# Cross-attention in float32: the output product as three single-pass products of upper parts, remainders and scaled differences

## The chip, the cores and the metric

One core of a Trainium2 chip runs the whole kernel. The metric is device microseconds of one execution, as the median of several. The kernel before takes 573.02 us (three runs, 572.77 to 575.41).

## The reference, cut to what matters

Everything is float32. The input x is (2, 2048, 640), the context is (2, 128, 384) with 124 text tokens and 4 adapter tokens for each of the two batches, and there are 8 heads of 80.

```python
query = hidden_states @ Wq
keyt, valt = enc @ Wk, enc @ Wv
hs = _mha(query, keyt, valt)                      # text attention
ca_q1 = jnp.einsum('btc,th->bch', ca, Wq_ca)[:, indices, :]
ca_hs1 = _mha(ca_q1, residual, residual)          # 384 adapter queries over 2048 tokens
ca_q2 = ca_hs1 @ Wq
ca_hs2 = _mha(ca_q2, ca @ Wk_ca, ca @ Wv_ca)
out = (hs + ca_hs2) @ Wout + b_out + residual
```

The change is in `hs @ Wout`: 4096 rows by 640 by 640. The adapter's part of the output product and the bias are made apart, as rows o2 of 384 for each batch, and gathered onto the output rows by an indirect DMA that adds.

## The kernel before, in words

**Units and stages.** The 4096 tokens are eight blocks of 512 for the queries and sixteen units of 256 (two tiles of 128) for everything behind. For unit m, `text_scores` (L2140) makes the scores sc, `softmax` (L2178) the probabilities, which go to HBM (kept) and come back turned, as pT (`probabilities`, L2242). `hidden` (L2365) multiplies pT with the values into PSUM (ph): the attention output of 256 tokens, turned, so that its 640 features lie on the partitions in five chunks of 128. `text_out_fast` (L2392) copies ph to SBUF (hs) and multiplies with Wout into PSUM (po). VectorE adds each finished half row of po (128x320) onto x, which `residual` (L2330) has loaded into a row tile. `stored` (L2508) lets GpSimd's queue gather-add the o2 rows (`add_second`, L2349) and then writes the rows to the output. `adapter` (L1869) runs beside this: for each batch 24 groups of scores s, of which VectorE takes the maxima mx, then 24 groups of scores whose exponentials ea ScalarE makes, contracted into acc (`contract`, L1985); `second` (L2030) ends it with o2.

**The output product before.** `by_columns` (L402) issues one 128-row product as four matmuls with weights of 128x32, one to each 32 columns of the array; they run at the same time. A float32 matmul is two matmul instructions in the trace. Of the five chunks of 128 features, four are multiplied by Winograd's form of Strassen's scheme: each unit has seven products of half size instead of eight. It needs sums of the hidden state (s1 to s4, written by VectorE or GpSimd into hs) and of Wout (t1 to t4, `sums_of_wout`, L2311). The seven products are 14 calls of `by_columns`, and the fifth chunk is 4 more: 18 for each unit. They stand in four chains, and eight adds of 128x320 on VectorE take them out.

**Who sets the order.** Every step is a `Do` that names its engine and its work. A class `Desk` (L67) issues the steps one by one in the order of a table, `TURNS` (L85): each task has a path of numbers, and each of its steps a turn. The remainder of a turn by 6 names the engine (0 TensorE, 1 ScalarE, 2 VectorE, 3 GpSimd, 4 SyncE, 5 none), and the turns count upwards through the program, so the turns divisible by 6, read in order, are TensorE's instruction stream. Each engine's queue runs strictly in that order. Path .55 is the adapter of the first batch, .55.1 that of the second (its end, `second`, is .55.1.3), and .56 to .71 are units 0 to 15; under a unit, .3 is `probabilities` with `hidden` in its last steps.

**Rooms.** A `Room` counts buffers; a step that needs one waits until it is free. Those of the late part: 4 PSUM banks m0 to m3 and 4 more (quad) for the adapter's scores; two rooms for pT, one in the slot of an old x block (`take_pT`, L2282); eight row tiles for x and the output rows (x_more and last_rows, `take_rows`, L2271); three sets for hs (`take_hs`, L2290).

**Shapes of the array.** Products with 128 rows and 32 columns (po, pq, ph, acc), 64 rows and 128 columns (sc), 32 rows and 128 columns (s) and the full 128 by 128 follow each other. The operands of s and of a part of sc are float32r (`F32R`), which is one matmul instruction for each product, on operands cut to fewer bits.

## Time and profile before

| | |
|---|---|
| time, median of 3 | 573.02 us |
| span of the profiled execution, first to last instruction | 571.3 us |
| its own time | recorded only as the span; the median is 1.7 us above it |
| TensorE busy | 563.6 us (99%) in 8069 matmul instructions |
| VectorE, ScalarE, GpSimd busy | 394.4, 286.7, 159.8 us |
| granted TensorE clock | 1.000 |
| DMA | 113.21 MB, mean 198 GB/s |

How to read it: a busy TensorE row says that matmul instructions follow each other without a gap, and their modelled ends overlap. What one product costs is the distance from its start to the start of the next, which the timeline shows, not the duration in a group's row. A row of the groups reads: line, engine, operation, output<-inputs, shape, count | busy us, mean ns of one | idle us before it and what ended it. The 128*32 ahead of a matmul's operands is the part of the array that it uses.

### The profile page before, as it was taken

The numbers are of one execution on the slowest core, as the hardware profiler recorded it, in microseconds if no ns is written. First come the engines' busy times: TensorE is split into PE (matmuls) and PEld (weight loads), VectorE is DVE, ScalarE is ACT, GpSimd is POOL, SyncE is SP. The second block draws the span as 40 slices with busy tenths as digits, with TensorE's granted clock in tenths as the row PEclk, the third lists the DMA queues.
The fourth block names the chain that finished last, engine by engine and source line by source line (L and its number), as shares of the span: only waits on it lengthen the run. The fifth ranks groups of instructions, "written<-read, shape, count | busy, mean of one in ns | idle before, by whom it ended". The sixth has DMA issues, their size and how long they took to land.

```text
span 571.3 us, 18875 instructions
## 1 busy us (share of the span) xinstructions
PE 563.6 (99%) x8069; PEld 310.0 (54%) x8069; DVE 394.4 (69%) x659; ACT 286.7 (50%) x806; POOL 159.8 (28%) x213
## 2 busy tenths in 40 slices
PE   9999999999999999999999999999999999999997
PEld 8885335455555455466554554554555554445553
DVE  4366999999998577458999999998332213544443
ACT  2021355645566899899876654524554664100000
POOL 9102041114440731100004350531203053045152
PEclk9999999999999999999999999999999999999999
DMA  8998576965968977446746969977476587799888
GB/s 246 211 248 126 139 161 157 172 179 139 211 212 153 215 182 211 146 126 198 233 158 203 316 180 319 245 217 230 96 263 120 164 206 223 248 211 213 258 156 237
DMA packets 145691, 113.21 MB, mean 198 GB/s; under 512 B 82548, under 2 KB 116980, under 8 KB 145608
## 3 DMA queue, kind: packets, MB, share of 16 engines
q1 hardware_dynamic: 137000, 95.10, 60.0%
q0 software_dynamic: 5632, 10.69, 11.7%
q10 hardware_dynamic: 2976, 6.23, 3.2%
q8 instruction: 63, 1.03, 0.8%
q14 instruction: 20, 0.16, 0.1%
HBM read 71.60 MB, written 40.39 MB: 196 GB/s over the span
## 4 chain that ended last, share of the span: by engine, by line
PE 92%; DVE 3%; ACT 3%; DMA 1%; issue 1%; SPq 0%; ACTq 0%; DVEq 0%
PE po L405 27%; PE pq L405 24%; PE sc L396 7%; PE acc L396 7%; PE s L396 7%; PE ph L396 6%; PE pq L396 4%; PE pyz L396 2%; ACT ea L427 2%; DVE mx L427 2%; PE pv L396 1%; PE pk L396 1%; DMA xz<-in_x_dram 1%; ACT p L427 1%; PE pt_wq L410 1%
## 5 line engine op out<-in xcount | busy, mean ns | idle before, releaser
L427 ACT ACTIVATE p<-sc,m 128x124 f32<-128x124 f32 x256 | 90.1, 381 | 43.4 <-DVE m L427 38.4
L427 DVE TENSOR_REDUCE mx<-s 128x4 f32<-128x2048 f32 x48 | 109.0, 2271 | 1.9 <-PE s L396 1.9
L427 ACT ACTIVATE ea<-s 128x2048 f32<-128x2048 f32 x48 | 90.5, 1884 | 31.4 <-PE s L396 30.9
L405 PE MATMUL po<-wout_sums,hs 128*32 128x320 f32 x1024 | 78.5, 434 | 0.1
L405 PE MATMUL po<-wout_sb,hs 128*32 128x320 f32 x928 | 72.4, 433 | 0.0
L427 POOL TENSOR_TENSOR p<-p,r 128x992 f32<-128x992 f32 x17 | 31.4, 1847 | 130.9 <-DVE r L427 130.9
L405 PE MATMUL pq<-xt,wq_sb 128*32 128x256 f32 (+1 forms) x928 | 66.4, 418 | 0.0
L427 DVE TENSOR_TENSOR last_rows<-last_rows,po 128x320 f32<-128x320 f32 x60 | 28.1, 480 | 44.0 <-PE po L405 43.9
L427 ACT ACTIVATION_READ_ACCUMULATOR p<-sc,m 128x1 f32 x256 | 57.0, 223 | 0.0
L427 DVE TENSOR_TENSOR x_more<-x_more,po 128x320 f32<-128x320 f32 x68 | 32.4, 481 | 34.5 <-PE po L405 32.5
L405 PEld LDWEIGHTS po<-wout_sums,hs 128*32 128x32 f32 x1024 | 33.4, 110 | 32.7 <-issue 2.8
L427 DVE TENSOR_REDUCE m<-sc 128x4 f32<-128x496 f32 x64 | 40.8, 663 | 14.1 <-PE sc L396 14.0
L396 PE MATMUL acc<-ea,y_sb 128*32 128x384 f32 (+2 forms) x768 | 50.2, 382 | 0.2 <-ACT ea L427 0.2
L396 PE MATMUL ph<-pT,vpad 128*32 128x256 f32 x768 | 47.9, 381 | 0.0
L405 PEld LDWEIGHTS po<-wout_sb,hs 128*32 128x32 f32 x928 | 30.1, 110 | 28.2 <-issue 1.6
L2351 POOL DMA_INDIRECT x_more<-o,query x17 | 26.6, 1563 | 67.0 <-DVE x_more L427 31.1
L405 PEld LDWEIGHTS pq<-xt,wq_sb 128*32 128x32 f32 x928 | 27.7, 110 | 28.0 <-issue 13.4
L427 ACT COPY hs<-ph 128x512 f32<-128x512 f32 (+1 forms) x25 | 13.4, 551 | 57.7 <-PE ph L396 57.7
L427 DVE STREAM_TRANSPOSE eb<-p 128x1024 f32<-128x1024 f32 x32 | 39.4, 1233 | 1.2 <-POOL p L427 1.1
L396 PEld LDWEIGHTS sc<-kmain,q 64*128 64x128 f32 x512 | 31.8, 187 | 12.6 <-issue 5.8
L427 POOL TENSOR_TENSOR hs<-hs 128x256 f32<-128x256 f32 x31 | 28.9, 1019 | 33.9 <-ACT hs L427 25.6
L396 PE MATMUL sc<-kmain,q 64*128 64x124 f32 x512 | 38.0, 285 | 0.0
(219 smaller groups left out, 835.0 us busy)
## 6 DMA issues: line engine op xcount, KB each, us to landing
kept<-eb SPq DMA_DIRECT2D x32, 512.0 KB
pT<-kept SPq DMA_DIRECT2D x16, 1024.0 KB
landing<-away SPq DMA_DIRECT2D x15, 512.0 KB
xi<-in_x_dram SPq DMA_DIRECT2D x56, 128.0 KB
x_more<-in_x_dram SPq DMA_DIRECT2D x17, 320.0 KB
last_rows<-in_x_dram SPq DMA_DIRECT2D x15, 320.0 KB
y<-yt SPq DMA_DIRECT2D x16, 256.0 KB
y_sb<-y SPq DMA_DIRECT2D x32, 128.0 KB
```

The costliest lines, as they stand in the source:

```text
L396: self.pin(self.nc.tensor.matmul(out, lhsT, rhs, **kw))
L405: self.pin(self.nc.tensor.matmul(out[j : j + 32], lhsT[:, j : j + 32], rhs, **kw))
L410: self.pin(self.nc.tensor.transpose(out, in_, ident))
L427: self.pin(getattr(engine, what)(*args, **kw))
L2351: desk.pin(nc.gpsimd.indirect_dma_start(out=t, out_offset=None, in_=o2_of[b], in_offset=bass.IndirectOffsetOnAxis(ap=query[:, st : st + 1] ...
```

## The change

The output product of a tile k of 128 tokens is now made with float32r matmuls on the full array. The hidden state a is split into an upper part h (its low 12 bits cleared) and the remainder l = a - h, and Wout the same way into wh and wl. With e = 2^-12, three products are summed: h·wh and l·(wl/e) into one PSUM bank, and (e·h - l)·(e·wh - wl) into another. VectorE adds (1 + e) times the first and -1/e times the second onto the row tile, which is h·wh + h·wl + l·wh + l·wl.

For each unit that is 2 tiles x 2 halves of the columns x 5 chunks x 3 products = 60 matmuls of 128x128 weights and 320 columns; a chain's step e0 has ten of them, its step e1 five. Ahead of them stand, for each of the two tiles, a masking on VectorE, two copies on ScalarE (one scaled) and two subtractions of 128x640 on GpSimd or VectorE; the sums s1 to s4 go. `parts_of_wout` replaces `sums_of_wout`: it loads the five chunks of Wout twice more and splits them.

Rooms: one for pT instead of two; five row tiles instead of eight; a room for the raw hidden state (raws); four sets of 128 tokens for h, l and e·h - l.

The first 190 turns of the table stay as they are, and all behind them is new. Four lines of the new table, for units 10, 11 and the second adapter's end (under a unit, .1 are its two row loads, .3 pT and hidden, .3.7, .3.8, .3.10, .3.11 the chains with steps e0 and e1, .3.12 and .3.13 the stores):

```
".55.1.3": [12638, 12643, 12650, 12696, 12703, 12713, 12720, 12785, 12786, 12857, 12863, 12935]
".66.1": [12742, 13192]   ".66.3": [10433, 12389, 12436, 12504, 12540, 12678]
".66.3.7": [13020, 13092]   ".66.3.8": [13062, 13098]   ".66.3.10": [13194, 13230]   ".66.3.11": [13200, 13206]
".67.1": [13396, 13702]   ".67.3": [12203, 12767, 13036, 13038, 13044, 13056]
```

The core of the diff:

```diff
@@ Desk
-            self.issue(max(self.ready(op), self.free[engine], self.now), engine, op)
+            self.issue(max(self.ready(op), self.free[engine]), engine, op)
+    def most(self, dst, src):
+        self.pin(self.nc.vector.tensor_scalar(dst.bitcast(U32), src.bitcast(U32), MOST, None, ALU.bitwise_and))
+    def less(self, dst, x, y):
+        (self.g_tensor_tensor if self.engine == "POOL" else self.v_tensor_tensor)(dst, x, y, ALU.subtract)
+    def scaled(self, dst, src, factor):
+        self.a_activation(dst, src, AF.Copy, scale=factor)
@@ rooms
     def take_pT():
-        op = yield Do("NONE", lambda z: z[0], [("x", B - 1, NSB - 1)], needs=[(xslots, 1)])
-        spare["pT"] = op.value
-        pTs.at.append(op.at.t)
         yield Do("NONE", lambda: None, ["last query"] + [("away", 2 * n + 1) for n in range(len(blocks))])
         pTs.at.append(desk.now)
+    def take_rows():
+        yield Do("NONE", lambda: None, ["last query"])
+        rows_of_tile(const.tile([P, NCH, P], F32, tag="wq4", name="x_last").rearrange("p c n -> p (c n)"), 1)
+        yield Do("NONE", lambda z: rows_of_tile(slot(z[0], "x_more", [P, 4 * H]), 4), needs=[(xslots, 1)])
+    def parts_of_wout():
...
+        for c in range(NCH):
+            yield Do("SP", lambda c=c: load(c), rank=3)
+            yield Do("DVE", lambda: desk.most(raw, raw), rank=3)
+            yield Do(EITHER, lambda c=c: copy(h[:, c], raw), marks=[("oh", c)], rank=3)
...
+    def parts_of_chunk(c, h, l, m):
+        op = yield Do("ACT", lambda: desk.scaled(m, h, EPS), [("oh", c)], rank=0)
+        op = yield Do(("POOL", "DVE"), lambda: desk.less(m, m, l), [op.at, ("or", c)], marks=[("om", c)], rank=0)
+        yield Do("ACT", lambda: desk.scaled(l, l, 1.0 / EPS), [op.at], marks=[("ol", c)], rank=0)
@@ text_out_fast
+        def split(k):
+            raw, most = [raws[0].tile[:, k, e] for e in range(2)]
+            op = yield Do("DVE", lambda: desk.most(most, raw), [("hsT", m, c0) for c0 in (0, 2, 4)], rank=1)
...
+                copy(sets[k][0][:, 0], most)
...
+            op = yield Do("ACT", lambda: desk.scaled(s, most, EPS), [h_at], rank=1)
+            op = yield Do(("POOL", "DVE"), lambda: desk.less(l, raw, most), [h_at], marks=[("hl", m, k)], rank=1)
+            yield Do(("POOL", "DVE"), lambda: desk.less(s, s, l), [s_at, l_at], marks=[("hm", m, k)], rank=1)
+        def chain(k, u):
+            cols = slice(u * HALF, (u + 1) * HALF)
+            for e in range(2):
+                def product(z, e=e):
+                    to, of = bank(z[0], f"po_{m}_{k}_{u}_{e}")[:, :HALF], sets[k][0]
+                    w_h, w_l, w_m = wout_parts
+                    for c in range(NCH):
+                        pairs = ((of[:, 2, c], w_m[c]),) if e else ((of[:, 0, c], w_h[c]), (of[:, 1, c], w_l[c]))
+                        for i, (x, y) in enumerate(pairs):
+                            matmul(
+                                to, x, y[:, cols], start=c == 0 and i == 0, stop=c == NCH - 1 and i == len(pairs) - 1
+                            )
...
+                def add(e=e, po=op.value):
+                    t = xr_of[m][k][0][:, cols]
+                    desk.b_scalar_tensor_tensor(t, po, -1.0 / EPS if e else 1.0 + EPS, t, ALU.mult, ALU.add)
```

## The prediction

> **What bounds the kernel now.** I read the page first, then who waited for whom on TensorE, then the groups kept apart by shape, and last the timeline where the output product runs alone.

> ```profile
> span 571.3 us, 18875 instructions
> PE 563.6 (99%) x8069; PEld 310.0 (54%) x8069; DVE 394.4 (69%) x659; ACT 286.7 (50%) x806; POOL 159.8 (28%) x213
> ...
> PE   9999999999999999999999999999999999999997
> ...
> PEclk9999999999999999999999999999999999999999
> ...
> PE 92%; DVE 3%; ACT 3%; DMA 1%; issue 1%; SPq 0%; ACTq 0%; DVEq 0%
> ```
> ```profile
> PE unread L396 <- DVE zeros L427: 1.1, 1, 1.1
> PE s L396 <- DVE mx L427: 1.1, 2, 0.7
> PE s L396 <- ACT ea L427: 0.6, 3, 0.2
> ```

> The chain that ended last is 92% TensorE, in every slice it is full at a full clock, and its longest waits on others come to 3 us. So the time is the sum of TensorE's passes and of what lies between them: a change gains what it takes from that sum and loses what it makes TensorE wait. The new output product touches three terms: the passes, the changes of the array's shape, and waits.

> **Term 1, the passes.**

> ```profile
> L405 PE MATMUL po<-wout_sums,hs 128*32 128x320 f32 x1024 | 78.5, 434 | 0.1
> L405 PE MATMUL po<-wout_sb,hs 128*32 128x320 f32 x928 | 72.4, 433 | 0.0
> L405 PE MATMUL po<-wout_sb,wout_sums 128*32 128x320 f32 x352 | 31.2, 433 | 0.0
> ```
> ```profile
> 514.34 2.34 PE L405 MATMUL po<-wout_sums,hs 128*32 128x320 f32 x32
> 516.49 0.83 PE L396 MATMUL ph<-pT,vpad 128*32 128x256 f32 x12
> ```

> The three groups hold 2304 instructions, which is 16 units x 18 calls x 4 columns x 2 instructions of a float32 product. Thirty-two of them, four calls, take 516.49 - 514.34 = 2.15 us, so a call is 0.5375 us, one of its two instructions 0.269 us, and the output product 288 x 0.5375 = 154.8 us. That is what goes.

> What comes is 16 x 60 = 960 float32r matmuls of 320 columns on the full array. No such matmul is in the trace. The nearest rows are the adapter's scores, float32r on 32-row tiles, four at a time:

> ```profile
> L396 PE MATMUL s<-zop,cop 32*128 32x512 f32 x192 | 24.3, 495 | 1.3 <-DVE mx L427 1.1 <-ACT ea L427 0.2
> ```
> ```profile
> 138.72 0.51 PE L396 MATMUL s<-zop,cop 32*128 32x512 f32 x4
> 139.15 1.06 PE L405 MATMUL pq<-xt,wq 128*32 128x512 f32 x8
> ```

> 48 groups of scores with four tiles are 192 instructions: a float32r product is one instruction. A visit of 512 columns takes 0.43 us, with two changes of shape in it. What those cost I take from the two products for w2, which go from 128x32 weights to full ones and back:

> ```profile
> 66.37 1.48 PE L396 MATMUL pw<-wout_sb,blk_v 128*32 128x320 f32 x10
> 67.78 1.06 PE L405 MATMUL pq<-xt,wq_sb 128*32 128x512 f32 x8
> ```
> ```profile
> L396 PE MATMUL pw<-wout_sb,blk_v x20: 432/432/537, 64.5 to 67.4; 128*32 128x320 f32 x16, 128*128 128x320 f32 x4
> ```

> From 66.37 to 67.78 there are two calls' worth of float32 work (eight narrow instructions and two full ones), 1.08 us at the price above, in 1.41 us: 0.33 us for entering the full shape and leaving it again. The first matmul in a shape takes 537 ns where the others take 432: 0.105 us is the load of its weights, which nothing hides. The remaining 0.2 us are two drains of about 0.1. A visit of s pays one load and one drain itself, so 0.43 - 0.105 - 0.1 = 0.23 us is left for 512 columns, 0.45 ns a column. At the 0.84 ns a column of a float32 instruction (0.269 us for 320) the columns alone would take 0.43 us and leave nothing for load and drain. So 320 columns take about 0.146 us.

> The weights of the next product have to be loaded within that time. The first query block shows how fast full weights can follow each other:

> ```profile
> 5.89 1.06 PE L396 MATMUL pq<-xt,wq_sb 128*128 128x128 f32 x8
> 6.78 0.39 PE L396 MATMUL unread<-zeros 128*128 128x128 f32 x2
> ```

> Eight instructions with 128 columns of weights each take 0.89 us, 0.111 each, so loads are hidden at 0.146. The new product is 960 x 0.146 = 140.2 us, and term 1 is 140.2 - 154.8 = **-14.6 us**. Its bounds from the rows: 0.111 us each, if only the loads set the pace (106.6 us, -48), and 0.269, if a float32r pass streams like a float32 one (258 us, +103). I take 0.146, since the scores are the only float32r rows whose columns, not loads, set the time.

> [...]

> **Term 2, the shapes.** po used to share the shape of pq, ph and acc. Reading the turns divisible by 6 out of both tables, in order, and giving each step its shape, I count 257 stretches of one shape before and 279 after: the 128 product steps stand in 40 stretches, often between scores, where one change replaces another. Each further stretch costs a load of 0.105 and a drain of 0.1: 22 x 0.205 = **+4.5 us**. The bounds are nothing, if the exchange hides in stretches that already paid, and 40 x 0.33 = 13.2 us, if every visit pays in full.

> **Term 3, waits.** What each engine gains or loses for one unit, from these rows:

> ```profile
> L427 ACT COPY o<-po 128x640 f32<-128x640 f32 x4 | 2.8, 693 | 7.2 <-PE po L396 6.7 <-DVE o L427 0.5
> L427 ACT ACTIVATE ea<-s 128x2048 f32<-128x2048 f32 x48 | 90.5, 1884 | 31.4 <-PE s L396 30.9
> L427 DVE TENSOR_TENSOR x_more<-x_more,po 128x320 f32<-128x320 f32 x68 | 32.4, 481 | 34.5 <-PE po L405 32.5 <-PE s L396 1.6
> L427 POOL TENSOR_TENSOR wout_sums<-wout_sb,wout_sums 128x640 f32<-128x640 f32 x2 | 3.1, 1542 | 5.7 <-DVE wout_sums L427 5.6
> L2351 POOL DMA_INDIRECT x_more<-o,query x17 | 26.6, 1563 | 67.0 <-DVE x_more L427 31.1 <-DVE r L427 15.3 <-DMA o<-o 14.1
> ```

> ```profile
> 501.39 2.77 PE L396 MATMUL ph<-pT,vpad 128*32 128x256 f32 x48
> 503.99 1.26 PE L405 MATMUL po<-wout_sums,hs 128*32 128x320 f32 x16
> ```
> ```profile
> 478.97 0.56 PE L396 MATMUL s<-cop,zop 32*128 32x128 f32 x8
> ...
> 479.64 1.88 ACT L427 ACTIVATE ea<-s 128x2048 f32<-128x2048 f32 x1 [1.77 <-PE s L396]
> ```

> ScalarE gets four copies of 128x640, 4 x 0.69 = 2.8 us; GpSimd at most four subtractions, 4 x 1.54 = 6.2, beside two gather issues, 3.1; VectorE keeps eight adds, gets two maskings (each at most two of its 0.48 us adds) and loses its share of the sums. A unit has 60 x 0.146 = 8.8 us of products and 2.6 of hidden (501.39 to 503.99) on TensorE, so none of these engines is full. From the end of hidden to the first product there is a copy out, a masking, a ScalarE copy and a subtraction, about 0.7 + 0.9 + 0.7 + 1.5 = 3.8 us; the new table puts products of the unit before into that time.

> In the second adapter a round of scores lasts at least the 1.88 us of ea and the 0.67 to reach it, 2.55. Adding up the new table's steps between one round and the next, 19 of the last 23 rounds hold over 2.8 us of TensorE work and four about 2.3: 1 us is lost there. Splitting Wout is 30 operations of 0.7 to 1.5 us, spread through the queries' part on engines that wait elsewhere, and ten more loads; the products need them only behind the last query, so I put nothing. Were it late, the products would be late by as much.

> The tail has no cover. There are five row tiles and one pT room:

> ```profile
> 493.63 0.81 PE L396 MATMUL po<-w_sb,p2T 32*128 32x320 f32 x4
> 498.48 1.55 POOL L2351 DMA_INDIRECT x_more<-o,query  x1 [14.06 <-DMA o<-o]
> 503.75 0.34 ACTq L447 DMA_DIRECT2D out_dram<-x_more  x1
> 508.99 0.33 SPq L447 DMA_DIRECT2D x_more<-in_x_dram  x1
> ```
> ```profile
> 542.57 0.33 SPq L447 DMA_DIRECT2D x_more<-in_x_dram  x1
> ```
> ```profile
> 549.00 1.55 POOL L2351 DMA_INDIRECT x_more<-o,query  x1 [4.98 <-DMA x_more<-in_x_dram]
> ```
> ```profile
> 494.00:571.00 77.00, 73.14 (x1116) 39.07 (x1112) 31.57 (x72) 3.41 (x6) 29.21 (x22) 1.00 0.87 221
> ```
> ```profile
> pT<-kept SPq DMA_DIRECT2D x16, 1024.0 KB
> ```

> From the adapter's last product a row tile needs 4.9 us to its gather, 5.3 more to its store, and another 5.2 to the next load: 15.4 before the load itself, which took up to 6.4 (issued at 542.57, waited for until 549.00). In the new table the adapter's last product is turn 12786; the second row of unit 10 is loaded at 13192, into the first tile that comes free, and its product is 13194. Between them TensorE has 6 e0 steps (1.46 each), 8 e1 steps (0.73), one hidden (2.6) and its shapes (0.3), 17.5 us. The tile is there after 15.4 and a load of 3 or more: TensorE waits 1 us or more, and its queue with it. Ten more tiles are turned round like that in a tail of 78 us of TensorE work (28 e0, 30 e1, five hidden, some shapes), so a tile has 5/11 of the 60 us between the first load and the last, 27 us. The parts of its round are a load (3 to 6.4), products (4.4, or 8.8 where two tiles alternate), an add (0.5), 5.3 and 5.2: 18 to 26 us. The tail moves the same 16 gathers and three more pT loads of 1 MB: the 17.0 MB (221 GB/s in 77 us) become about 20. I take **+3 us** for all waits, between 0 and 10.

> **The sum.** -14.6 + 4.5 + 3 = -7.1 us: a span of 564.2 for 571.3, and with the 1.7 us to the median **565.9 us** for 573.02.

> **The rivals.**
> - *Tiles run short, slower.* Place: the tail's loads of x. If a tile's turn lasts longer than the 27 us that the products leave it, each us more costs 2.2, since 11 loads go through five tiles; with the DMA at a share of 0.87 already and a fifth more to move, the slow end of 26 and two waits in SyncE's or GpSimd's queue make 33 us possible: +13 us, 576 (573.0 - 14.6 + 4.5 + 13). It makes the kernel slower from 32 us on. Against it: 18 to 26 us from the rows. Chance 0.10.
> - *The gain is eaten, no change.* Every visit to the full shape pays 0.33 (13.2 us): 573.0 - 14.6 + 13.2 = 571.6; or the tail waits 8 us: 571. Chance 0.14.
> - *Columns at full pace.* If a float32r column costs half of a float32 instruction's 0.84 ns, 0.42, a product is 0.136 us with a little between; 960 x 0.136 = 130.6 us, and 573.0 - 24.2 + 4.5 + 3 = 556. For it: the visit of scores would then hold 0.22 us of load and drain, hardly more than I took off, and weights can follow each other at 0.111. Against: 0.45 by that row. Chance 0.12. [...]
> - *Not one pass.* A full-array float32r product streams at 0.84: 573.0 + 103 + 4.5 = 681. Against it: the score visit has no room for that. Chance 0.03.

> **How the numbers follow.** The forecast has the remaining 0.61; a difference of 0.5%, 2.9 us, is about what a measurement of this kernel can tell from none. Faster by more: forecast and full pace, 0.73. Within: 0.14. Slower: short tiles and two-pass, 0.13. The forecast's own range is 561 (no waits) to 570; the range of 8 in 10 reaches down to the full pace and up into the short tiles, 555 to 577.

> **What would show it.** The po group: 960 instructions of 128x128 weights and 320 columns, ten of them 1.46 us apart from the next step. TensorE's idle by cause: right, if it is under 6 us and lies behind the loads of rows after the adapter's end. Wrong: po starts 0.136 or 0.27 us apart; a stretch of po costing far more than its matmuls and 0.33; idle before s or ph, from ScalarE or GpSimd, through the middle.

## The result and the profile after

| | before | after |
|---|---|---|
| time, median | 573.09 us (572.77 to 575.41) | 594.43 us (590.69 to 602.10) |
| ratio | | 1.0343, 95% interval 1.031 to 1.0376 |
| profiled execution, its span | 573.02, 571.3 us | 590.69, 589.0 us |
| mean granted clock of that execution | 1.000 | 0.989 |

The kernel is slower by 3.4%. The slow execution of 602.10 us (mean clock 0.976) is set aside; the ratio is that of the other three, and their median, 592.51 us, is what the experiments below are held against. Forecast were 565.9 us and a range of 555 to 577: the time is outside it, on the other side of before.

The page of the kernel after, its busy row, its slices and the engines on the chain that ended last:

```profile
span 589.0 us, 16397 instructions
PE 560.5 (95%) x6725; PEld 378.9 (64%) x6725; DVE 417.4 (71%) x684; ACT 324.1 (55%) x844; POOL 226.7 (38%) x237
...
PE   9999995999999999989999899999899999998996
...
PEclk9999997999999999999999999999999999999999
...
PE 34%; DVE 6%; DMA 6%; ACT 2%; issue 2%; SPq 1%; POOL 0%; ACTq 0%; DVEq 0%; POOLq 0%
```

TensorE's busy time went down by 3.1 us and the span up by 17.7. TensorE is no longer full in every slice, one slice has only half, and there the granted clock is lower too. The chain is no longer 92% TensorE. The waits of TensorE say who it waits for now (us in total, times, the longest):

```profile
PE s L441 <- DVE mx L478: 9.5, 5, 6.2
PE s L441 <- ACT ea L478: 3.3, 7, 1.5
PE ph L441 <- DMA pT<-kept: 2.4, 2, 2.1
PE po L441 <- DVE wout_fifth L478: 2.2, 2, 1.8
```

Scores that waited 1.1 and 0.6 us for mx and ea now wait 9.5 and 3.3. The third row is the tail, the fourth a chain that waits for its split hidden state (the fourth set of h, l and e·h - l lies in the tile wout_fifth).

**The new product.** The timeline of TensorE where a chain follows hidden, and the groups of po:

```profile
540.57 2.80 PE L441 MATMUL ph<-pT,vpad 128*32 128x256 f32 x48 [2.06 <-DMA pT<-kept]
543.30 0.41 PE L441 MATMUL po<-wout_h,hs 128*128 128x320 f32 x1
543.55 0.31 PE L441 MATMUL po<-wout_l,hs 128*128 128x320 f32 x1
543.69 0.31 PE L441 MATMUL po<-wout_h,hs 128*128 128x320 f32 x1
```
```profile
L441 PE MATMUL po<-wout_h,hs 128*128 128x320 f32 x220 | 66.6, 316 | 0.0
L441 PE MATMUL po<-wout_l,hs 128*128 128x320 f32 x176 | 52.0, 307 | 0.0
```

From one product to the next it is 0.14 to 0.15 us; over all stretches of po it is 0.147. The duration of 307 to 316 in the groups' rows is not that price: two products overlap. The first in a new shape holds 0.25 before the next can start, 0.10 more: the load of its weights starts together with it (543.30), where that of the next product starts 0.14 ahead of it (543.40 for 543.55).

**By stage.** To see where time went, I gave each instruction of TensorE the distance to the next start that its form has in undisturbed stretches, and each change of shape a load and a drain. The sum is TensorE's work; what the starts need beyond it is lost. Both are estimates, worked out from the starts in the trace. Before: 557.6 us of work, 8.0 lost. After: 548.3 of work, 33.4 lost, and the stretch behind the last start grew from 4.6 to 6.2. So the work fell by 9.3 us, and 25.4 us of waits and of slower clock came in. (The waits that the profile lists add up to 22.1 us after and 3.5 before. With 3.6 us at half clock, below, that is 22.2 of the 25.4; the rest lies in shorter gaps or in the error of the estimate.)

| us of the span | 0-60 | 60-120 | 120-280 | 280-345 | 345-480 | 480-end |
|---|---|---|---|---|---|---|
| lost after | 3.1 | 9.9 | 4.1 | 6.1 | 4.8 | 5.4 |

Before, 2.5 of the 8.0 us lie in the first 20 us and 1.9 in 280 to 345.

**The half-empty slice.** Timelines of SyncE, GpSimd, VectorE and TensorE of the kernel after (start, length, engine, operation, idle time before it and what ended it):

```profile
83.70 1.15 SPq L512 DMA_DIRECT2D wout_raw<-in_L_xattn_Wout_dram  x2
84.95 0.58 SPq L512 DMA_DIRECT2D y<-yt  x1
85.57 1.30 SPq L512 DMA_DIRECT2D away<-first_rests  x2
```
```profile
90.22 1.28 POOL L478 TENSOR_TENSOR x_sums<-xt 128x512 f32<-128x512 f32 x1 [21.10 <-DMA away<-first_rests]
91.46 1.84 POOL L478 TENSOR_TENSOR p<-p,r 128x992 f32<-128x992 f32 x1
```
```profile
93.33 1.25 DVE L478 STREAM_TRANSPOSE eb<-p 128x1024 f32<-128x1024 f32 x1 [7.93 <-POOL p L478]
...
95.72 2.28 DVE L478 TENSOR_REDUCE mx<-s 128x4 f32<-128x2048 f32 x1
```
```profile
89.14 2.76 PE L456 MATMUL pq<-xt,wq 128*32 128x512 f32 x24
98.06 0.80 PE L441 MATMUL s<-zop,cop 32*128 32x512 f32 x4 [6.17 <-DVE mx L478]
```

Read it from the end. Scores wait 6.17 us for a maximum. VectorE takes that maximum late, since its queue stands for 7.93 us at the transpose of p. p is late since GpSimd's queue stands at a sum of x, which may overwrite first_rests only when the transfer "away" has read it. And that transfer is issued at 85.57, behind two of Wout's raw loads, a run of loads of x and a store of yt, which came 0.6 us ahead of it. Before the change the same transfer was issued early, and GpSimd's sum was done before anybody missed it:

```profile
63.59 1.18 SPq L447 DMA_DIRECT2D away<-first_rests  x2
```
```profile
71.41 1.27 POOL L427 TENSOR_TENSOR x_sums<-xt 128x512 f32<-128x512 f32 x1 [1.41 <-ACT rests L427]
```

Four queues, each strictly in order, pass one late transfer on to TensorE. Then comes a second price. The busy times by stretch of the kernel after (after the comma: PE, PEld, DVE, ACT, POOL; then the granted clock):

```profile
86.00:91.30 5.30, 5.30 (x71) 2.08 (x64) 0.00 (x0) 1.94 (x9) 1.08 (x1) 1.00 0.41 124
91.30:95.00 3.70, 0.60 (x8) 0.00 (x0) 1.67 (x2) 0.00 (x0) 3.62 (x4) 1.00 0.50 142
95.00:105.20 10.20, 6.70 (x40) 4.01 (x44) 10.20 (x15) 3.77 (x15) 3.95 (x3) 0.50 0.55 181
105.20:110.00 4.80, 4.80 (x74) 2.58 (x66) 2.91 (x7) 2.57 (x12) 0.00 (x0) 1.00 0.37 120
```

TensorE idles from 91.9 on, the clock halves at 95 and stays at 0.50 for 10.2 us. Work resumed at 98.06, so some 7.1 us ran at half pace: 3.6 us more. The stall costs about 6.2 + 3.6 us.

**The stages with the second adapter.** The same columns, kernel before and then after, for 280 to 345 us and 345 to 480:

```profile
280.00:345.00 65.00, 63.75 (x939) 33.97 (x941) 63.82 (x79) 41.87 (x163) 20.53 (x18) 1.00 0.68 209
345.00:480.00 135.00, 135.00 (x2085) 68.76 (x2081) 74.47 (x117) 69.65 (x125) 34.07 (x30) 1.00 0.76 212
```
```profile
280.00:345.00 65.00, 59.93 (x835) 37.21 (x827) 61.02 (x76) 52.23 (x151) 29.22 (x19) 1.00 0.71 225
345.00:480.00 135.00, 131.96 (x1463) 98.76 (x1462) 95.58 (x140) 86.05 (x163) 68.17 (x43) 1.00 0.78 217
```

Before, VectorE was busy for 63.82 of these 65 us: it was as full as TensorE. Over the span it has 69%, which hides this. So work that a change puts there should make the maxima late; these rows alone don't show it, since VectorE's busy time after is no longer, 61.02 us. Experiment 12 tests it. Behind, VectorE gets 21 us more in 135, and GpSimd twice its work.

### The profile page after: what moved, and what is told of

Its sections match the earlier page's. It is cut to its first block, busy times and chain, and to the rows that moved or that the text cites. A ratio compares the mean times of both kernels' runs of the same rounds, so it can differ in the third digit from the quotient of the medians.

```text
span 589.0 us, 16397 instructions
## 1 busy us (share of the span) xinstructions
PE 560.5 (95%) x6725; PEld 378.9 (64%) x6725; DVE 417.4 (71%) x684; ACT 324.1 (55%) x844; POOL 226.7 (38%) x237
## 4 chain that ended last, share of the span: by engine, by line
PE 34%; DVE 6%; DMA 6%; ACT 2%; issue 2%; SPq 1%; POOL 0%; ACTq 0%; DVEq 0%; POOLq 0%
PE po L441 20%; PE ph L441 5%; PE s L441 3%; DMA pT<-kept 3%; PE acc L441 2%; PE pq L456 2%; DVE mx L478 2%; ACT ea L478 2%; PE sc L441 2%; DMA x_last<-in_x_dram 1%; DMA out_dram<-x_more 1%; DMA x_more<-o,query 1%; SPq L512 1%; DVE m L478 1%; DVE eb L478 1%
## 5 line engine op out<-in xcount | busy, mean ns | idle before, releaser
L478 ACT ACTIVATE p<-sc,m 128x124 f32<-128x124 f32 x256 | 89.8, 376 | 21.3 <-DVE m L478 21.1
L478 POOL TENSOR_TENSOR p<-p,r 128x992 f32<-128x992 f32 x24 | 45.2, 1886 | 116.7 <-DVE r L478 114.9
L478 DVE SCALAR_TENSOR_TENSOR x_more<-po,x_more 128x320 f32<-128x320 f32 x104 | 47.9, 482 | 48.7 <-PE po L441 48.1
L441 PE MATMUL po<-wout_h,hs 128*128 128x320 f32 x220 | 66.6, 316 | 0.0
L2449 POOL DMA_INDIRECT x_more<-o,query x26 | 41.5, 1596 | 57.2 <-DVE x_more L478 49.2
L441 PE MATMUL po<-wout_l,hs 128*128 128x320 f32 x176 | 52.0, 307 | 0.0
L478 ACT COPY hs_raw<-ph 128x512 f32<-128x512 f32 (+1 forms) x32 | 15.8, 527 | 56.2 <-PE ph L441 56.1
L441 PEld LDWEIGHTS po<-wout_h,hs 128*128 128x128 f32 x220 | 41.3, 188 | 5.2 <-issue 3.0
L441 PEld LDWEIGHTS ph<-pT,vpad 128*32 128x32 f32 x768 | 24.0, 110 | 19.6 <-DMA pT<-kept 2.6
L478 POOL TENSOR_TENSOR hs<-hs_raw 128x640 fp32r<-128x640 f32 x14 | 23.2, 1656 | 33.8 <-DVE hs_raw L492 31.2
L456 PE MATMUL pq<-xt,wq 128*32 128x512 f32 x280 | 35.1, 614 | 0.1
## 6 DMA issues: line engine op xcount, KB each, us to landing
pT<-kept SPq DMA_DIRECT2D x16, 1024.0 KB
```

What stands on the lines that cost most here:

```text
L441: self.pin(self.nc.tensor.matmul(out, lhsT, rhs, **kw))
L456: self.pin(self.nc.tensor.matmul(out[j : j + 32], lhsT[:, j : j + 32], rhs, **kw))
L478: self.pin(getattr(engine, what)(*args, **kw))
L2449: desk.pin(nc.gpsimd.indirect_dma_start(out=t, out_offset=None, in_=o2_of[b], in_offset=bass.IndirectOffsetOnAxis(ap=query[:, st : st + 1] ...
```

## The experiments

Two theories at the start. **A**: the steps are right, but the new table has bad places in it, above all the late transfer; with better places the change wins. **B**: the splitting itself costs, by its operations on VectorE, GpSimd and ScalarE, by its loads, and by the rooms that its tiles take. A third question is what a stall costs beyond its own length.

### 1. The two transfers early

```diff
- ".8.5.5": [2056], ".8.5.6": [2062],
+ ".8.5.5": [1402], ".8.5.6": [1408],
```

> The changed kernel with two DMA issues moved forward on SyncE's queue: the first block's second half (away<-first_rests) stands ahead of the first load of Wout's parts instead of behind the second. Theory A, a queue held up: the second load of wout_raw waits for the raw tile, the two transfers behind it leave at 85.57 us instead of about 62, the GpSimd subtraction x_sums waits for them until 90.22, and p, eb, mx and s wait behind it; so the 6.17 us of idle TensorE at 91 us go, and with them about 3.6 us of matmuls at a granted clock of 0.5 behind it: 594.4 - 9.8 = about 584.6 us. Theory B, too much work on VectorE, ScalarE and GpSimd: the same wait comes back a little later, and at most 3 us go (591 or more).

Measured: 585.27 us (583.07 to 591.35), ratio 1.0229 [1.0156, 1.0302], where the kernel after has 592.51. The long wait is gone; the maxima are now waited for in five short pieces:

```profile
PE s L441 <- DVE mx L478: 4.3, 5, 1.4
PE ph L441 <- DMA pT<-kept: 3.5, 3, 2.1
PE po L441 <- DVE wout_fifth L478: 2.1, 2, 1.8
PE sc L441 <- DVE q L478: 1.7, 1, 1.7
```

By the medians, two numbers of the table were worth 7.2 us, where 9.8 were expected. The size is uncertain, since these four executions alone scatter by 8 us. That the stall is gone is not: it was a place in a queue and not more work. Part of the gain was lost again: a new wait of 1.71 us, on q at 249 us, was followed by 6.83 us at half clock, and 1.7 + 3.4 us went there. 12.2 us over before remain.

### 2, 6, 7. What a stall costs, in the kernel before

GpSimd's first sum of x is repeated, so that TensorE idles at that place in a kernel without the change.

```diff
-                (desk.g_tensor_tensor if desk.engine == "POOL" else desk.v_tensor_tensor)(w[:, i], x, y, ALU.subtract)
+                for _ in range(14 if (n, i) == (2, 0) else 1):
+                    (desk.g_tensor_tensor if desk.engine == "POOL" else desk.v_tensor_tensor)(w[:, i], x, y, ALU.subtract)
```

> The kernel before, with GpSimd held for about 17 us at 71 us by repeating its first x_sums subtraction 13 more times (the output stays as it is). Nothing of the change is in it. Theory A: p comes at about 92 us as in the changed kernel, TensorE idles for some 6 us before an s, the granted clock then falls to 0.5 for about 10 us, and the kernel takes 573.1 + 6.2 + 3.6 = about 583 us (579 to 586). If the low clock of the changed kernel belongs to its new products and not to the idle time, the clock stays at 1.0 and only the idle time is added (579). If TensorE has other work at that place in this order, nothing is added (573 to 575).

The other two have 9 and 7 in place of 14.

> The kernel before with GpSimd held by 8 repeats of its first x_sums subtraction instead of the 13 of the run before this one (1.37 us each). There TensorE idled for 12.1 us before an s and the granted clock was 0.5 for 13.65 us. Here the idle time should be 12.1 - 5 x 1.37 = about 5.3 us, as long as the one of the changed kernel at 91 us (6.2). If an idle time of that length lowers the clock without anything of the change in the kernel: 573.1 + 5.3 + 2 to 4 = 580 to 583 us, with a stretch of granted clock 0.5 in the trace. If not: 578 to 579 us.

> The kernel before with 6 repeats: idle time of about 12.1 - 7 x 1.37 = 2.5 us. In the changed kernel waits of 1.5 to 2.1 us passed without a lower clock, and in the run with the early transfer one of 1.7 us was followed by 6.8 us at 0.5. If 2.5 us are enough: 573.1 + 2.5 + 2 to 4 = 577.5 to 579.5 us. If not: 575.6 us.

The wait in the three, 14, 9 and 7 times, in that order:

```profile
PE s L396 <- DVE zop L427: 12.1, 1, 12.1
```
```profile
PE s L396 <- DVE zop L427: 6.1, 1, 6.1
```
```profile
PE s L396 <- DVE zop L427: 2.3, 1, 2.3
```

| repeats | time us | over before | idle | half clock |
|---|---|---|---|---|
| 14 | 586.61 (586.00 to 587.04) | 13.5 | 12.1 | 13.65 |
| 9 | 581.54 (580.39 to 582.00) | 8.1 | 6.1 | 6.83 |
| 7 | 578.02 (576.34 to 580.67) | 4.6 | 2.3 | 3.41 |

Each costs more than its idle time, by 1.4 to 2.3 us, and in each the clock halves for one, two or four times 3.41 us. The part of it in which TensorE had work again counts half: with 14 repeats it idled from 85.9 to 98.0 and the half clock ran from 88.0 to 101.6; 3.7 us of it had work, so 1.8 were lost, and 12.1 + 1.8 = 13.9 against 13.5 measured. With 9, the half clock ran from 89.8 to 96.6 and work from 92.3: 6.1 + 2.2 = 8.3 against 8.1. With 7 repeats all 3.41 us had work: 2.3 + 1.7 = 4.0 against 4.6. One execution with 7 repeats kept a mean clock of 1.000 and took 576.34, the others had 0.993 to 0.997. So even 2.3 us of idle can halve the clock, and doesn't always.

### 3. Wout not split

One chunk of Wout is loaded and copied; the remainders and scaled differences are left out, and all three products use the upper part.

```diff
-            yield Do("SP", lambda c=c: load(c), rank=3)
-            yield Do("DVE", lambda: desk.most(raw, raw), rank=3)
+            yield Do("SP", lambda c=c: None if c else load(c), rank=3)
+            yield Do("DVE", lambda c=c: None if c else desk.most(raw, raw), rank=3)
...
-        op = yield Do("ACT", lambda: desk.scaled(m, h, EPS), [("oh", c)], rank=0)
+        op = yield Do("ACT", lambda: None, [("oh", c)], rank=0)
```

> The changed kernel without the splitting of Wout: only the first of its five chunks is loaded and masked, the other four copies of upper parts read the same tile, and the second loads, the remainders and the scaled differences are left out; all three products take the same upper part, as many matmuls as before. Theory A: no load waits for the raw tile, so the 9.8 us at 91 us go, and the 2.2 us in which po waits for wout_fifth at 418 us: about 582.4 us, and up to 3 us less if the remainders on GpSimd and the scalings on ScalarE also hold the adapter's rounds at 259 to 297 us. Theory B: under 3 us go.

Measured: 591.86 us (587.94 to 595.30), 1.0329 [1.0271, 1.0387]. I had thought that Wout's second load was what kept the transfer back. It was not:

```profile
84.02 0.57 SPq L512 DMA_DIRECT2D y<-yt  x1
84.64 1.29 SPq L512 DMA_DIRECT2D away<-first_rests  x2
```
```profile
PE s L441 <- DVE mx L478: 6.2, 4, 3.8
```

Without Wout's second load ahead of it the transfer is still issued at 84.64, only 0.9 us earlier: it stands behind the loads of x and the store of yt, and SyncE's queue gets to it no sooner. It also lands sooner, 3.1 us after its issue instead of 4.6 (GpSimd goes on at 87.72 instead of 90.22). The stall is 3.8 us instead of 6.2, and the half clock lasts 10.24 us all the same. Of the 6.2 us, 2.4 go with Wout's loads; 3.8 are the place in the queue. The times of the two kernels overlap.

### 4. The hidden state not split

The masking, the scaled copy and the subtractions are left out; all three products use one and the same copy of the hidden state.

```diff
-            op = yield Do("DVE", lambda: desk.most(most, raw), [("hsT", m, c0) for c0 in (0, 2, 4)], rank=1)
+            op = yield Do("DVE", lambda: None, [("hsT", m, c0) for c0 in (0, 2, 4)], rank=1)
...
-            op = yield Do(("POOL", "DVE"), lambda: desk.less(l, raw, most), [h_at], marks=[("hl", m, k)], rank=1)
+            op = yield Do(("POOL", "DVE"), lambda: None, [h_at], marks=[("hl", m, k)], rank=1)
```

> The changed kernel without the splitting of the hidden state: it is copied once by ScalarE, and the masking, the scaled copy and the two subtractions of each tile are left out; all three products read the copy, as many matmuls as before. Theory A: the stall at 91 us stays; of the rest only the waits at 322, 329 and 334 us (1.4 + 1.6 + 1.0) and those of the tail at 557 to 560 us (1.0 + 0.6) are within its reach: 594.4 - 4 = about 590, with 5.6 at most. Theory B, the vector engines are what sets the time in the second half: 10 us or more go.

Measured: 590.40 us (587.88 to 594.26), 1.0325 [1.0273, 1.0377]. The lost time falls from 33.4 to 30.9 us. The waits at 329, 418 and 557 us go, and new ones on pT, 1.5 and 1.6 us, come at 365 and 561. The times overlap with those of the kernel after, so this edit is better judged in 12.

### 5 and 8. Two other orders

The kernel of experiment 1, its steps, engines and rooms, with another table from turn 1140 on. Unit 10 as a sample, 5 and then 8:

```diff
- ".66.1": [12742, 13192], ".66.3": [10433, 12389, 12436, 12504, 12540, 12678],
+ ".66.1": [7804, 8092], ".66.3": [7373, 7583, 7624, 7704, 7782, 7788],
```
```diff
- ".66.1": [12742, 13192], ".66.3": [10433, 12389, 12436, 12504, 12540, 12678],
+ ".66.1": [7798, 8146], ".66.3": [5993, 7613, 7648, 7788, 7794, 7806],
```

> The changed kernel with another table of turns and nothing else: every step, its engine, its instructions, the rooms and the sizes stay as in the changed kernel, and only the order in each engine's queue differs, from turn 1140 on. The new order leaves more time between the landing of a transfer and the steps queued behind the one that needs it; the order of the products of each block of queries is kept. Theory A, the products and the shape changes cost what was priced (-9.3 us together by the trace of the changed kernel) and the loss is waits that the new table made: nearly all of the waits behind 60 us go, the granted clock stays at 1.0 to the tail, and the kernel takes 566 to 571 us, 2 to 7 us under the kernel before. Theory B, the fewer rooms and the work of splitting on VectorE, ScalarE and GpSimd hold TensorE whatever the order is: 580 us or more.

> A third order of the changed kernel's steps, again with the same engines, instructions, rooms and sizes, planned with more time for the transfers of the second half: in the second order (588 us, profiled 583.2 us of span) TensorE lost 28.9 us beside its work, 24 of them behind 300 us, where VectorE waited up to 3.8 us for the row loads and ScalarE 3.5 us for a gathered row before a store. Theory A, only the order of the queues is at fault: the loss behind 300 us falls to about 14 us and the kernel takes 576 to 579 us. Theory B, the five row tiles and the one room for pT hold the second half in any order: 583 to 588 us.

Measured: 587.97 us (583.74 to 591.44), 1.0252 [1.0209, 1.0295], and 587.57 (586.12 to 588.62), 1.0251 [1.0234, 1.0268]. Neither beats the 585.27 of the table that they replaced. In 0 to 280 us they lose 5.2 and 4.8 us, hardly more than the 4.3 of before. In 280 to 345 they lose 7.3 and 10.3, in 345 to 480 us 6.3 and 8.5, behind it 10.2 and 5.4. What these orders save in one stage comes back in another, so these two orders don't bear theory A out in its general form: beyond the late transfer, the loss is not just that table's.

The longest waits of TensorE in the first of the two, experiment 5:

```profile
PE ph L445 <- DVE x_more L482: 5.4, 2, 3.4
PE s L445 <- DVE mx L482: 4.4, 6, 1.8
PE po L445 <- POOL hs L482: 2.5, 1, 2.5
```

The first row is two waits. The longer, 3.45 us from 529.58 on, is the tail that I had named: VectorE's add into a row waits 3.76 us for the load of x, and hidden waits behind it. The other, 1.92 us until 407.33, is not: there an add stands in VectorE's queue behind a product of p with r that is slow beside a subtraction on GpSimd. In the third row, at 557.97, a subtraction gets its input late, since ScalarE's queue stood 3.54 us at a store whose gathered row hadn't landed. Timelines of GpSimd and VectorE ahead of 407.33:

```profile
403.68 2.13 POOL L482 TENSOR_TENSOR hs<-hs 128x640 fp32r<-128x640 f32 x1
```
```profile
403.54 3.34 DVE L482 TENSOR_TENSOR p<-p,r 128x992 f32<-128x992 f32 x1
```

The median of VectorE's products of p with r in the kernel before is 1.19 us. GpSimd's 2.13 us show no slowing: the same subtraction takes 2.13 us at 425.95 in the kernel after, where VectorE starts nothing for its first 1.84 us.

### 9 to 12. Taking the costs off one after the other

Each is the one before with one thing more. 9: experiments 1 and 3 together.

> Both earlier edits at once, as the base for the next run: the first block's second half leaves early, and Wout is not split (one chunk loaded, no remainders, no scaled differences, all three products take the upper part). The order is the changed kernel's. The first edit alone gave 585.3 us, the second alone took 2.6 us off 594.4. If the splitting of Wout costs nothing once its second load blocks nobody: 583 to 586 us; if it loads the vector engines so that TensorE waits: 579 or less.

10: the memory of Wout's remainders and scaled differences, free in 9, becomes a second room for pT and four more row tiles.

```diff
-            "NONE", lambda z: xrow.tile([P, 4 * H], F32R, tag="xz", name="wout_l"), ...
+            "NONE", lambda z: rows_of_tile(xrow.tile([P, 4 * H], F32, tag="xz", name="x_rows"), 4), ...
-            "NONE", lambda z: slot(z[0], "wout_m", [P, 4 * H], F32R), [("x", B - 1, NSB - 1)], needs=[(xslots, 1)]
+            "NONE", lambda z: second_pT(z[0]), [("x", B - 1, NSB - 1)], needs=[(xslots, 1)]
```

> The run before this one with more rooms, in the memory that the remainders and scaled differences of Wout no longer take: a second room for pT and four more row tiles (nine for five). Order, engines and instructions are as there. Theory B, the rooms are what TensorE waits for in the second half: the waits of ph for pT (0.35 + 1.1 + 1.9 + 0.5 + 2.6 = 6.4 us in the run without Wout's splitting) go and it is 5 to 8 us faster than the run before this one. Theory A, the order: at most 2 us faster, since the queues still issue in the old order.

11: 10 with the table of experiment 8.

> The third order with the added rooms and without Wout's splitting: the run of the third order and the one with more rooms put together. Theory B: the loss behind 300 us falls below 10 us and the kernel takes 567 to 573 us, no slower than the kernel before. Theory A: as the third order by itself, within 3 us.

12: 11 with the edit of experiment 4.

> The run with the third order, the added rooms and without Wout's splitting (572.7 us, granted clock 1.0, 16.6 us lost beside TensorE's work against 8.0 in the kernel before), now also without the splitting of the hidden state: one copy by ScalarE instead of a masking, two copies and two subtractions; as many matmuls as before, all on the same copy. In that run 7.0 us of the loss lie between 280 and 345 us, where the kernel before loses 1.8 us and has VectorE busy for 63.8 of 65 us. Theory A, VectorE is full there and every addition to its queue becomes a wait of TensorE: the loss of that stretch falls to 2 to 4 us and the kernel takes 566 to 569 us, 4 to 7 us under the kernel before. Theory B, the waits there belong to the order of the adapter's rounds and not to the added work: 571 to 573 us.

| kernel | time us | ratio to before | lost us | of it 280-345 |
|---|---|---|---|---|
| after | 592.51 | 1.0343 [1.031, 1.0376] | 33.4 | 6.1 |
| 1 transfers early | 585.27 | 1.0229 [1.0156, 1.0302] | 29.5 | 5.9 |
| 9 and Wout not split | 582.80 | 1.0155 [1.0138, 1.0173] | 25.5 | 6.9 |
| 10 and more rooms | 577.99 | 1.0081 [1.0056, 1.0105] | 18.3 | 4.7 |
| 11 and another order | 572.69 | 0.9984 [0.9974, 0.9994] | 16.6 | 6.9 |
| 12 and hidden not split | 568.41 | 0.9921 [0.9905, 0.9936] | 11.7 | 4.7 |

(Lost time is that of the profiled execution. That of the kernel after was 1.8 us under its median and that of experiment 1 was 1.7 us above, so the first step looks smaller in it than in the times.)

The steps are 7.2, 2.5, 4.8, 5.3 and 4.3 us. Each kernel was timed beside the kernel before, not all at the same time; by the ratios the steps are 6.5, 4.2, 4.2, 5.6 and 3.6 us. The first two aren't well told apart, since the interval of experiment 1 alone is 8 us wide. They are also the steps of this sequence; another might share them out otherwise. Against what was expected, 9 comes out at the edge of the 583 to 586 us for a splitting of Wout that costs nothing by itself, 10 gives a little less than the 5 to 8 us of the rooms, and 11 and 12 fall into their ranges. The order that gave nothing with few rooms (587.57 against 585.27) gives 5.3 us with more: what an order is worth depends on the rooms. The two stretches of 12, to be held against those of before:

```profile
280.00:345.00 65.00, 61.33 (x777) 39.67 (x771) 60.90 (x75) 40.80 (x135) 8.92 (x5) 1.00 0.72 224
345.00:480.00 135.00, 134.29 (x1518) 98.91 (x1520) 74.28 (x117) 78.39 (x131) 28.53 (x18) 1.00 0.78 216
```

The second row of 11:

```profile
345.00:480.00 135.00, 133.12 (x1483) 97.83 (x1481) 88.55 (x133) 89.68 (x148) 65.28 (x41) 1.00 0.76 211
```

With nothing split TensorE is nearly full in 345 to 480 us, and VectorE's busy time there is 74.28 us, which is that of before, where 11 has 88.55. In 280 to 345 us 4.7 us are still lost, where 2 to 4 were expected: leaving the split out takes 2.2 us off that stretch, and s still waits 2.8 us for maxima there, with VectorE busy for 60.90 of 65 us. So VectorE's added work is part of that loss and not all of it; what the rest hangs on, no run tells.

Only 12 is clearly faster than before, by 4.4 us; 11 is level with it. With all of these costs off, 568.41 us lies in the forecast's own range of 561 to 570. But 12 leaves the splitting of both operands out, and 9 to 11 that of Wout, so none of them computes what the reference asks for. A version that does, and that beats before, I didn't find: the rooms of 10 lie in memory that Wout's remainders and scaled differences need.

## Why the prediction was wrong, point by point

**Term 1, the passes: right.** 0.147 us a product where the prediction took 0.146, by scores of another shape; 960 of them make 141 us, and 140.2 were forecast. Two rivals fall with it: full pace (0.136, an estimate that no run shows) and two passes (0.269).

**Term 2, the shapes: right.** 0.10 for the load by the rows above, some 0.09 for the drain (a last product holds 0.24 before the next shape can start), and 282 changes of shape in the trace where before has 261: 21 more for 22 counted. The part of the rival in which every visit pays 0.33 falls with it. Terms 1 and 2 together were -10.1; by the trace the work fell by 9.3.

**Term 3, the waits: wrong, and nearly the whole error.** The step as it was put: "I take **+3 us** for all waits, between 0 and 10." The trace has 25.4, clock included: 22.4 of the 24.8 us by which the span missed the forecast. Three statements under it failed.

- "Splitting Wout is 30 operations of 0.7 to 1.5 us, spread through the queries' part on engines that wait elsewhere, and ten more loads; the products need them only behind the last query, so I put nothing." It asked when the products need Wout, not what stands behind Wout's loads and beside them. The new table brought "away" from 63.59 us to 85.57, behind Wout's loads, loads of x and a store. The transfer frees a tile without any room that says so, so nothing in the table shows that GpSimd, VectorE and TensorE hang on it. The stall cost 6.2 + 3.6 us by the trace, and experiment 1, without it, is 7.2 us faster. Splitting Wout beyond that is worth 2.5 us in 9, within the scatter of 1.
- "so none of these engines is full": the sums were per unit and against TensorE's time for that unit. But the second adapter's maxima run in the same stretch, and VectorE was full there before the change (the rounds with ea were priced, at 1 us, those with mx not): 63.82 of 65 us in the trace of before. Splitting the hidden state, put at nothing, cost 4.3 us (11 to 12; 3.6 by the ratios). By the lost time 2.2 of it lie in that stretch. VectorE's slowness beside GpSimd has a part in the kernel after (1.84 us in one place, below); its share here isn't measured.
- The tail, with "five row tiles and one pT room", was seen as the only place without cover. The rooms did cost, 4.8 us and then 5.3 through the order that they allow, but the waits weren't only there: 480 us to the end lost 5.4 us of the 33.4.

**A cost with no place in the sum.** Every wait was priced at its length. But the clock fell to half for 10.24 us behind the stall of 6.17 us in the kernel after, which cost 6.2 + 3.6 us, and for 6.83 us behind the 6.1 us of experiment 6, which cost 8.1.

**The rival on the slower side** put the tail at 13 us with five tiles. The mechanism is real (experiment 5 has a wait of 3.4 us on it), but it isn't what made this kernel slow, so the chance of 0.13 for slower was too low for the wrong reason as well. The prediction's sign of being wrong, "idle before s or ph, from ScalarE or GpSimd, through the middle", is what the waits show, with VectorE in the place of ScalarE in most of it.

**Open.** Whether one order with five row tiles and one room for pT can gain: two others than the kernel's didn't, which proves nothing of the rest. And why s still waits for maxima in 280 to 345 us with nothing split, where 4.7 us are lost and before lost 1.9.

## What to carry to other kernels

Where TensorE is full, the gain of fewer passes is easy to count and the loss is in the waits: price the added work stage by stage against the busy time of each engine in that stretch, not against its share of the span. When an order is rewritten, look for the transfers that have moved late and ask what each of them frees, above all memory that two tiles share. And a stall of TensorE can cost more than its length, since the clock may drop behind it: 2.3 us of idle time cost 4.6 here, 6.1 cost 8.1 and 12.1 cost 13.5.

## What the runs showed of the hardware

**The clock after a stall.** The granted clock fell to half behind these idle times of TensorE: 6.17 us in the kernel after (for 10.24 us), 12.1, 6.1 and 2.3 us in experiments 2, 6 and 7 (for 13.65, 6.83 and 3.41), 1.71 us in experiment 1, from 249.21 on (for 6.83). That is 3.41 us once, twice, three and four times. It fell 2.1 us after TensorE had gone idle in experiment 2 (85.9 to 88.0), 3.1 in the kernel after (91.9 to 95.0) and 3.6 in experiment 6 (86.2 to 89.8); in experiment 7 TensorE was busy again by then. The length alone doesn't decide: the 1.71 us of experiment 1 were enough, while 3.45 us in experiment 5, from 529.58 on, were not, and one of the seven executions of experiment 7 kept a mean clock of 1.000.

**Kernels with many waits scatter more.** The four executions of experiment 1 lie between 583.07 and 591.35 us at mean clocks of 0.990 to 0.995. The ten of experiment 11, at 0.998 to 1.000, lie between 571.73 and 573.92.

**VectorE beside GpSimd.** In the kernel after, a masking of 128x640 takes 0.45 us alone and 1.60 beside a subtraction that GpSimd began 0.3 us before it; GpSimd's 1.55 us are its usual time (median 1.57). The other way round little is lost: where the masking begins 0.16 us before the subtraction (357.95, 403.51 and 516.74 us), it keeps 0.47 to 0.49 us and the subtraction takes 1.75 to 1.78. Timelines of VectorE and GpSimd of the kernel after:

```profile
328.20 0.45 DVE L492 TENSOR_SCALAR hs_raw<-hs_raw 128x640 uint32<-128x640 uint32 x1
328.57 2.28 DVE L478 TENSOR_REDUCE mx<-s 128x4 f32<-128x2048 f32 x1
330.77 1.60 DVE L492 TENSOR_SCALAR hs_raw<-hs_raw 128x640 uint32<-128x640 uint32 x1
```
```profile
328.72 1.56 POOL L478 TENSOR_TENSOR wout_fifth<-hs_raw 128x640 fp32r<-128x640 f32 x1 [1.90 <-DVE hs_raw L492]
330.47 1.55 POOL L478 TENSOR_TENSOR wout_fifth<-wout_fifth 128x640 fp32r<-128x640 f32 x1 [0.18 <-ACT wout_fifth L478]
```

The maxima between them keep their 2.28 us with GpSimd at work. It can reach TensorE: at 416.80 a masking takes 2.53 us beside GpSimd, VectorE comes to the subtraction behind it only at 419.66, and the products that need it wait 1.84 us. In experiment 5 a product p<-p,r takes 3.34 us beside a subtraction on GpSimd, where the median in the kernel before is 1.19. By what VectorE is held up there, no run shows.
